# D * u added on GpSimd instead of by a transpose, and some loads asked for at other slots, in a Mamba layer with an FFN

## The chip, the cores and the metric

The kernel runs on one core of a Trainium2 chip. The metric is the device time of one execution in microseconds (us). TensorE is PE in the profile (PEld is its weight load), VectorE is DVE, ScalarE is ACT, GpSimd is POOL, and SyncE is SP, whose queue issues the DMAs.

## What is computed

Two sequences of 4096 tokens with 512 channels go through a Mamba layer and then an FFN with 4-bit weights, each with a layer norm before and after and a residual. The part that the change touches is the end of the Mamba layer:

```
h_in, gate = split(x_norm @ in_proj)                      # I = 1024 each
u   = silu(causal_conv(h_in) + conv_b)
ts, B, C = split(u @ x_proj, [128, 144])                  # N = 16 states
dt  = softplus(ts @ dt_proj + dt_b)
h_t = exp(dt * A) * h_(t-1) + dt * u * B                  # per channel and state
y   = sum over the 16 states of (h * C) + D * u
out = (y * silu(gate)) @ out_proj
```

All is float32 (matmuls in a mode in which two rounded halves of each operand are used, three products for one).

## The kernel before, in words

**Two stages.** The first stage, up to about 985 us, does the norm, in_proj, the convolution, x_proj and dt, group by group of 512 tokens (16 groups), and writes to device memory what the second needs: dt and D * u by channel (`dd_d`), dt * u with time on the partitions (`dT_d`), B, C, and silu(gate) (`g_d`; a part of the gates is left for the second stage, with inputs in `xg_d` and weights in `wg_d`).

**Slots.** The second stage is written as a list of slots. Time is cut into segments of 63 steps; a chunk is 4 segments, but the first chunk of each of the two sequences has one segment. A unit is one chunk for one block of 128 channels (8 blocks, `ib`). A unit has 2 slots for each segment, one for each half (`hf`) of the 16 states: 8 slots, or 2 in a one-segment chunk; 2080 slots in all. In a slot:

- TensorE makes the input of the scan two slots ahead, `make_b` (L938), two matmuls of the tile d (dt * u, from `dT_d`) with Bd, a diagonal matrix of B values that GpSimd makes (`make_bd`, L806). It goes into one of two PSUM tiles;
- ScalarE makes exp(dt * A) for the next unit (`make_exp`);
- VectorE runs the scan (L967), after a copy of the carried state (L966);
- after every second segment, GpSimd multiplies the states with C into `pr` (L979), 128 channels x 8 states x 126 steps, one product for each half of the states. h has two tiles, pr four;
- four slots later, `nsum` (L985) sums the states on TensorE: each of the 8 states of the half is transposed into the same PSUM tile yp and adds up there (L999), 16 transposes for both halves. A seventeenth (L1002) adds D * u, the tile du. VectorE multiplies with the gate (L1005), and the result goes to `y_d`.

**Beside the scans.** Matmul work runs between the slots: for each group of 512 tokens, out_proj of one group and the FFN of the one before (in the first two groups, the rest of the gates). `tail` yields it in small steps. A counter `pe` adds up an estimate of TensorE's time, and after each slot the loop takes steps until the counter has reached the slot's share of the group's `cost`; what is left at the end of the group is taken at once. An ordinary group has 128 slots:

```
cost += length * (2 * TB + (2 * NH + 1) * TT / NU)
...
while g >= 0 and pe[0] < cost * (slot + 1 - start[g]) / length and next(todo, 0) is None:
    pass
```

Here NH is 8, NU is 4, TB = 0.125, TT = 0.107, TM = 0.235 us. The group with the batch boundary in it has 144 slots.

**Order.** The order on PE, ACT, POOL and SP is that of the program; only VectorE's is chosen by the scheduler.

**Loads.** Functions handed to `at(slot, f)` run at that slot. `unit_steps` (L866) asks for dt and d of unit m at the slot in which unit m - 2 begins. In a one-segment chunk four units share a load; units 4 to 7 (`ib == NU`) of the second sequence's are asked for at the last unit of the chunk before, those of the very first chunk fall under the general rule. `load_gate` (L876) asks for du and the gate of unit k + 3 four slots after the last sum of unit k. `gates(hf, ...)` (L1025) asks for its 8 weight tiles of 256 KB at its start; `following` are the first loads of the next group's out_proj.

Of the kernel before, what the change touches and what calls it, by code (L numbers as in the profile page):

```python
# [25 lines left out]
def kernel(  # L26
# [7 lines left out]
    nc = tc.nc  # L34
# [7 lines left out]
    KH, KI, KF = H // P, I // P, HID // P  # L42
# [14 lines left out]
    NU = 4  # L57
# [648 lines left out]
    with ExitStack() as sb:  # L706
# [44 lines left out]
        NH = N // 2  # L751
# [14 lines left out]
        def first_of(c):  # L766
            nb, q, _ = chunks[c]
            return nb * T + V * q
# [97 lines left out]
        def unit_steps(m):  # L866

            b, n = (slots[m - 2], slots[m - 1] - slots[m - 2]) if m > 1 else (0, 0)
            c, ib = units[m]
            if chunks[c][2] == 1 and c and ib == NU:  # L870
                b, n = slots[c * KI - 1], NU * 2
            at(b, lambda: load_dt(m))
            for i in range(4):
                at(b + (1 + i if n > 2 else i // 2), lambda i=i: load_t4(m, i // 2, i % 2))
# [48 lines left out]
                nc.scalar.activation(dA[2 * (k % 2) + hf][:, :n_, m, 1:U], dtv, AF.Exp, scale=A[:, ib, n:n + 1])  # L923

        YA = 2
        prods, summed = {}, set()
        NE = 1
        hs = {}

# [22 lines left out]
        def scan(k, u, hf, slot):  # L952
            c, ib = units[k]
            q, n_ = chunks[c][1:]
            Cb = chunk[c][2]
            j, uu = divmod(u, 2)
            dAt = dA[2 * (k % 2) + hf]
            if hf == 0:
                hs["prev"] = last[ib] if u == 0 else hs["h"][:, :, 1 - uu, :, U - 1]
                if uu == 0:  # L960
                    hs["h"] = hp.tile([P, 2, 2, NH, U], F32, name=f"h{k}_{j}", tag="h")
            h = hs["h"][:, hf]
            b = bt.pop(slot)
            with tc.high_priority(offset=HP):
                if q + u:
                    nc.vector.tensor_copy(b[:, :, 0], hs["prev"][:, hf])  # L966
                scans.append(nc.vector.tensor_tensor_scan(  # L967
                    h[:, uu].rearrange("p n t -> p (n t)"),
                    dAt[:, u].rearrange("p n t -> p (n t)"),
                    b.rearrange("p n t -> p (n t)"),  # L970
                    0.0, ALU.mult, ALU.add,
                ))
            if u == n_ - 1 and hf == 1:
                nc.gpsimd.tensor_copy(last[ib], hs["h"][:, :, uu, :, U - 1])
            if uu == 1 or u == n_ - 1:
                pr = prp.tile([P, NH, 2 * V], F32, name=f"pr{k}_{j}_{hf}", tag="pr")
                f = 1 if q + u else 0
                to = pr[:, :, :(uu + 1) * (U - f)].rearrange("p n (u t) -> p u n t", t=U - f)
                nc.gpsimd.tensor_mul(to, h[:, :uu + 1, :, f:], Cb[j, hf][:, :uu + 1, :, f:])  # L979
                prods.setdefault(k, []).append(pr)  # L980
                sums.append((slot + NS, k, j, hf))

# [2 lines left out]
        def nsum(k, j, hf):  # L985

            c, ib = units[k]
            du, gt = glane[k]
            t, m = windows(c)[j]
            o_ = t - first_of(c)  # L990
            if hf == 0:
                i = nsums[0] % YA if now[0] < start[1] - 1 else None
                nsums[0] += 1
                yps[k, j] = (ps_w if i is None else ps_a).tile([P, P], F32, name=f"yp{c}_{ib}_{j}", tag="w" if i is None else f"a{i + 4 - YA}")
            yp = yps[k, j]
            pr = prods[k].pop(0)
            pe[0] += (NH + hf) * TT
            for n in range(NH):
                nc.tensor.matmul(yp[:m], pr[:, n, :m], ident, is_transpose=True, start=(hf == 0 and n == 0), stop=False)  # L999
            if hf == 0:  # L1000
                return
            nc.tensor.matmul(yp[:m], du[:, o_:o_ + m], ident, is_transpose=True, start=False, stop=True)  # L1002
            del yps[k, j]
            yt = sm.tile([P, P], F32, name=f"yt{c}_{ib}_{j}", tag="yt")
            nc.vector.tensor_mul(yt[:m], yp[:m], gt[:m, j])  # L1005

            def store():
                for g, o, at_, w in pieces(t, m):
                    nc.sync.dma_start(y_d[g][ib, o:o + w, :], yt[at_:at_ + w])
                    if o + w == G:  # L1010
                        summed.add((g, ib))

            at(now[0] + YD, store)
            if j == len(windows(c)) - 1:
                del lane[k], glane[k], prods[k]
                at(now[0] + 4, lambda: load_gate(k + 3))
# [5 lines left out]
        NS = 4  # L1022


        def gates(hf, following):  # L1025

            w = [c1.tile([P, KH, 512], FR, name=f"wg{hf}_{e}", tag="xh" if e == 0 else "xl") for e in range(2)]
            for kt in range(KH):
                for e in range(2):
                    nc.sync.dma_start(f32(w[e][:, kt]), wg_d[2 * hf + e][:, kt])  # L1030
            if hf:
                yield

            def x_in(g, j):
                t = wn_.tile([P, 2, KH, P], FR, name=f"xg{hf}_{g}_{j}", tag="wn")
                nc.sync.dma_start(f32(t), xg_d[g][j - JS])
                return t

            todo_ = [(g, j) for g in range(GS, NG - 1) for j in range(JS, J)]
            held = []  # L1040

            def let_go(f):

                while f in held:
                    held.pop(0)()

            if not hf:
                pe[0] += GD[0]
                yield
            raw, nxt = [], [x_in(*q) for q in todo_[:1 + hf]]  # L1050
            pe[0] += GD[1 + hf]
            yield
            for i, (g, j) in enumerate(todo_):
                t = nxt.pop(0)
                if i == 0 and not hf:
                    nxt.append(x_in(*todo_[1]))
                if i >= len(todo_) - 2:
                    following.send(None)
                if len(held) > 1:
                    let_go(held[0])  # L1060
                pm = (ps_a if hf else ps_w).tile([P, 512], F32, name=f"pz{hf}_{g}_{j}", tag=f"a{i % J}" if hf else "w")
                for kt in range(KH):
                    mm3b(pm, t[:, 0, kt], t[:, 1, kt], w[0][:, kt], w[1][:, kt], kt == 0, kt == KH - 1)
                    yield
                    if kt == 1 and i + 2 < len(todo_):
                        nxt.append(x_in(*todo_[i + 2]))
                z = row(f"z{hf}_{g}_{j}")
                held.append(lambda z=z, pm=pm: nc.scalar.copy(z, pm))
                at(now[0] + 2, lambda f=held[-1]: let_go(f))
                raw.append((g, j, z))  # L1070
                if len(raw) == GB or i == len(todo_) - 1:
                    def silu(raw=raw):
                        let_go(held[-1] if held else None)
                        for _, _, z in raw:
                            nc.scalar.activation(z, z, AF.Silu)

                    def store(raw=raw):
                        for g_, j_, z in raw:
                            nc.sync.dma_start(g_d[g_][4 * hf:4 * hf + 4, j_ * P:(j_ + 1) * P, :].rearrange("k p i -> p k i"), z.rearrange("p (k i) -> p k i", i=P))

                    at(now[0] + 3, silu)
                    at(now[0] + 5, store)
                    raw = []
            let_go(held[-1] if held else None)
            ahead[hf] = following.send(None)
            yield
# [7 lines left out]
        def row(nm):  # L1094
            return c2.tile([P, H], F32, name=nm, tag="xn", bufs=RB)
# [19 lines left out]
        def early(g):  # L1115

            ys = y_in(g, 0)
            w = w_in(g, 0)
            yield
            yn = y_in(g, 1)  # L1120
            wn = w_in(g, 1)
            yield
            tp = y_turn(g, 0, ys)
            yield split(c2, tp, [P, J, P], f"yy{g}_0", nc.scalar.copy, tag="h", bufs=HB), [w, wn], [yn]
# [260 lines left out]
        def tail(p):  # L1385

            if p == 0:
                yield from gates(0, early(0))
                return
            t, beside, late = turned.pop(p - 2, []), [], None  # L1390
            if p >= 2 and not t:
# [3 lines left out]
            ff = ffn(p - 2, t, early(p) if p < NG else None) if p >= 2 else iter(())  # L1395
            if p - 1 < NG:
                acc = new_acc(f"ca{p}")
                late = gates(1, early(1)) if p == 1 else None
                if late:
                    next(late)  # L1400
                yield from out_proj(p - 1, acc, ahead.pop(p - 1), beside, ff)
                assert not beside
                state[p - 1] = []
                norms(p - 1, acc, state[p - 1])
# [146 lines left out]
```

## Time and profile before

| | us |
|---|---|
| median of 3 runs (4635.6 to 4637.55) | 4637.4 |
| the profiled execution | 4638.11 |
| its span, first to last instruction | 4636.2 |
| first stage | about 985 |
| an ordinary group of 128 slots | 209.7 |
| TensorE busy in each 100 us from 1500 to 4400 | 97 to 99.6, but 89.8 from 2700 to 2800 |
| mean granted TensorE clock | 0.992 |

The whole page shows one busy figure for each engine over the span. A row of groups has the line, engine, operation, output and inputs with shapes, the count, then busy time and mean ns of one, then the idle time before it and what ended it. In a timeline, the first two figures are the start and the length in us, and a bracket gives idle time just before the row and who ended it. In a row of windows there are the stretch, its length, and for each engine the busy time with the number of instructions, then the granted clock, the DMA share and GB/s.

Other rows of use: `L1002 PE MATMUL yp<-ident,du` ran 528 times, its weight load 138 ns in the median; DVE's scan takes 1220 ns, its copy 166 ns.

### The profile page before, as it was taken

How to read it: one execution, taken by the hardware profiler on the slowest of the kernel's cores; microseconds unless marked ns; L12 is line 12 of the kernel's file. 1: busy time of each engine (PE TensorE's matmuls, PEld its weight loads, DVE VectorE, ACT ScalarE, POOL GpSimd, SP SyncE). 2: the span in 40 equal slices, each digit the busy share in tenths (PEclk: the TensorE clock that was granted, in tenths of full speed). 3: DMA queues.
4: the chain of work that ended last, by engine and by line, in shares of the span. 5: the costliest groups of instructions: out<-in, count | busy, mean ns of one | idle time of the engine just before them, and what ended most of it. 6: DMA issues, size and time to landing. Idle time of an engine off the chain costs nothing.

```text
span 4636.2 us, 84785 instructions
## 1 busy us (share of the span) xinstructions
PE 4479.6 (97%) x26613; PEld 3867.9 (83%) x26613; DVE 3843.9 (83%) x6273; ACT 3306.1 (71%) x7321; POOL 3275.0 (71%) x2360
## 2 busy tenths in 40 slices
PE   8999999979899999999999989999999999999999
PEld 6777777768788888888888878888888888888887
DVE  6677777759889999999989989899999999999931
ACT  5777777777688776867677667777686767767643
POOL 1333333349788888889888888888898989888820
PEclk9999999989999999999999999999999999999999
DMA  4888888778889787978888877879798978888765
GB/s 149 260 254 259 261 259 255 232 218 223 243 232 257 223 248 211 260 216 255 221 245 232 232 204 222 240 223 252 211 265 217 255 221 249 231 232 243 212 235 195
DMA packets 1137329, 1083.91 MB, mean 234 GB/s; under 512 B 140599, under 2 KB 910415, under 8 KB 1136888
## 3 DMA queue, kind: packets, MB, share of 16 engines
q1 hardware_dynamic: 1136888, 1078.49, 80.6%
q8 instruction: 220, 3.60, 0.3%
q14 instruction: 221, 1.81, 0.1%
HBM read 800.87 MB, written 277.29 MB: 233 GB/s over the span
## 4 chain that ended last, share of the span: by engine, by line
PE 75%; DVE 6%; DMA 6%; POOL 5%; ACT 4%; issue 3%; SPq 1%; DVEq 0%; POOLq 0%; ACTq 0%
PE yp L999 15%; PE b L949 8%; PE pu L99 5%; PE pu L100 5%; PE pu L101 5%; PE fa L99 5%; PE fa L100 5%; PE fa L101 4%; DVE h L967 3%; POOL pr L979 3%; PE pm L100 2%; PE pm L99 2%; PE pm L101 2%; POOL bd L809 2%; PE ca L99 1%
## 5 line engine op out<-in xcount | busy, mean ns | idle before, releaser
L979 POOL TENSOR_TENSOR pr<-h,cb 128x1008 f32<-128x1008 f32 (+1 forms) x1056 | 2454.0, 2336 | 469.9 <-DVE b L966 313.9
L967 DVE TENSOR_TENSOR_SCAN h<-dA,b 128x512 f32<-128x512 f32 x2080 | 2536.2, 1220 | 128.4 <-PE b L949 9.8
L923 ACT ACTIVATE dA<-dt,A 128x252 f32<-128x252 f32 x4096 | 1702.0, 496 | 163.6 <-DVE h L967 143.1
L999 PE MATMUL yp<-ident,pr 128*126 128x128 f32 (+1 forms) x8448 | 1104.9, 274 | 18.2 <-DVE xl L1265 6.8
L999 PEld LDWEIGHTS yp<-ident,pr 128*126 128x126 f32 (+1 forms) x8448 | 950.4, 140 | 28.5 <-issue 11.7
L949 PEld LDWEIGHTS b<-bd,d 128*128 128x128 f32 x4160 | 752.7, 190 | 209.2 <-issue 27.1
L949 PE MATMUL b<-bd,d 128*128 128x256 f32 x4160 | 875.4, 291 | 48.6 <-DVE h L967 15.7
L1312 ACT ACTIVATE pu<-pu,bu 128x512 f32<-128x512 f32 x256 | 168.8, 659 | 602.5 <-PE pu L101 602.5
L437 DVE SCALAR_TENSOR_TENSOR pm<-hin,cw,pm 128x512 f32<-128x512 f32 x384 | 288.4, 751 | 210.0 <-ACT pm L434 203.0
L99 PE MATMUL fa<-wn,hh 128*128 128x512 f32 x1024 | 421.1, 411 | 0.0
L99 PE MATMUL pu<-xh,wu 128*128 128x512 f32 x960 | 401.7, 418 | 5.0 <-DMA wu<-wu_d 4.8
L100 PE MATMUL fa<-wn,hh 128*128 128x512 f32 x1024 | 403.6, 394 | 0.0
L101 PE MATMUL fa<-wn,hl 128*128 128x512 f32 x1024 | 401.0, 392 | 0.0
L100 PE MATMUL pu<-xl,wu 128*128 128x512 f32 x960 | 378.3, 394 | 0.0
L101 PE MATMUL pu<-xh,wu 128*128 128x512 f32 x960 | 375.8, 392 | 0.0
L433 POOL COPY halo<-hin 128x3 f32<-128x3 f32 x128 | 28.1, 219 | 461.8 <-ACT hin L432 461.8
L966 DVE COPY b<-h 128x8 f32<-128x8 f32 x1536 | 254.7, 166 | 108.1 <-PE b L949 101.6
L1316 DVE TENSOR_TENSOR hl<-pu,hh 128x512 fp32r<-128x512 f32 x256 | 172.1, 672 | 152.5 <-ACT hh L1314 152.5
L809 POOL TENSOR_TENSOR bd<-dl,bp 128x512 fp32r<-128x512 f32 x260 | 273.1, 1060 | 1.1 <-DMA bp<-B_d 1.1
L101 PEld LDWEIGHTS fa<-wn,hl 128*128 128x128 f32 x1024 | 192.3, 188 | 44.8 <-DVE hl L1316 0.6
L101 PEld LDWEIGHTS pu<-xh,wu 128*128 128x128 f32 x960 | 180.4, 188 | 42.0
L100 PEld LDWEIGHTS fa<-wn,hh 128*128 128x128 f32 x1024 | 193.8, 189 | 20.3
(582 smaller groups left out, 7786.9 us busy)
## 6 DMA issues: line engine op xcount, KB each, us to landing
d<-dT_d SPq DMA_DIRECT2D x1040, 128.0 KB
wu<-wu_d SPq DMA_DIRECT2D x256, 512.0 KB
wn<-wn_d SPq DMA_DIRECT2D x256, 512.0 KB
cb<-C_d SPq DMA_DIRECT2D x128, 512.0 KB
wo<-wo_d SPq DMA_DIRECT2D x128, 512.0 KB
dd_d<-du SPq DMA_DIRECT2D x128, 256.0 KB
dd_d<-v SPq DMA_DIRECT2D x128, 256.0 KB
ys<-y_d SPq DMA_DIRECT2D x128, 256.0 KB
```

The costliest lines, as they stand in the source:

```text
L99: nc.tensor.matmul(ps, ah, bh, start=start, stop=False)
L100: nc.tensor.matmul(ps, ah, bl, start=False, stop=False)
L101: return nc.tensor.matmul(ps, al, bh, start=False, stop=stop)
L437: cv = nc.vector.scalar_tensor_tensor(pm, hin[:, k:k + G], cw[:, ib, k:k + 1], pm, ALU.mult, ALU.add)
L809: nc.gpsimd.tensor_mul(tb, dl.unsqueeze(1).to_broadcast([P, N, 32]), bp[:, w // 2, w % 2, :].unsqueeze(2).to_broadcast([P, N, 32]))
L923: nc.scalar.activation(dA[2 * (k % 2) + hf][:, :n_, m, 1:U], dtv, AF.Exp, scale=A[:, ib, n:n + 1])
L949: nc.tensor.matmul(b[:, :, v * 32:(v + 1) * 32], t4[:, u if l is None else l, v, :], Bd[2 * u + v][:, hf * NH:(hf + 1) * NH, :], start=Tru ...
L966: nc.vector.tensor_copy(b[:, :, 0], hs["prev"][:, hf])
L967: scans.append(nc.vector.tensor_tensor_scan(h[:, uu].rearrange("p n t -> p (n t)"), dAt[:, u].rearrange("p n t -> p (n t)"), b.rearrange(" ...
L979: nc.gpsimd.tensor_mul(to, h[:, :uu + 1, :, f:], Cb[j, hf][:, :uu + 1, :, f:])
L999: nc.tensor.matmul(yp[:m], pr[:, n, :m], ident, is_transpose=True, start=(hf == 0 and n == 0), stop=False)
L1316: nc.vector.tensor_sub(hl, pu, f32(hh))
```

## The change

The loads: dt and d of units 4 to 7 of the very first chunk are asked for at slots 0 and 1, and those of the first two units after a one-segment chunk at units 2 and 4 of the short chunk instead of units 6 and 7. The gate weights are now asked for through a list of four parts: all at once for the first half, and for the second half one part at a time, handed to out_proj as `beside`. The first loads of the next group are sent for in the middle of the last two gate blocks instead of at their start.

The sum: where du of the unit is already asked for when the second half's product is made, GpSimd adds du to state 0 of that product, in place, and the transpose of du is left out. The `cost` of the pacing is not edited.

```diff
             c, ib = units[m]
-            if chunks[c][2] == 1 and c and ib == NU:
-                b, n = slots[c * KI - 1], NU * 2
+            if chunks[c][2] == 1 and ib == NU:
+
+                b, n = (slots[c * KI - 1], NU * 2) if c else (0, 0)
+            elif c and chunks[c - 1][2] == 1 and ib < 2:
+                b = slots[m - 6 + ib]
             at(b, lambda: load_dt(m))
...
                 nc.gpsimd.tensor_mul(to, h[:, :uu + 1, :, f:], Cb[j, hf][:, :uu + 1, :, f:])
+                if hf and k in glane:
+                    added.add((k, j))
+                    t_, m_ = windows(c)[j]
+                    o_ = t_ - first_of(c)
+                    nc.gpsimd.tensor_add(pr[:, 0, :m_], pr[:, 0, :m_], glane[k][0][:, o_:o_ + m_])
...
-            pe[0] += (NH + hf) * TT
+            own = hf and (k, j) not in added
+            pe[0] += (NH + own) * TT
             for n in range(NH):
-                nc.tensor.matmul(yp[:m], pr[:, n, :m], ident, is_transpose=True, start=(hf == 0 and n == 0), stop=False)
+                nc.tensor.matmul(yp[:m], pr[:, n, :m], ident, is_transpose=True, start=(hf == 0 and n == 0), stop=(hf == 1 and not own and n == NH - 1))
             if hf == 0:
                 return
-            nc.tensor.matmul(yp[:m], du[:, o_:o_ + m], ident, is_transpose=True, start=False, stop=True)
+            if own:
+                nc.tensor.matmul(yp[:m], du[:, o_:o_ + m], ident, is_transpose=True, start=False, stop=True)
...
-        def gates(hf, following):
+        def gate_weights(hf):
             w = [c1.tile([P, KH, 512], FR, name=f"wg{hf}_{e}", tag="xh" if e == 0 else "xl") for e in range(2)]
-            for kt in range(KH):
+
+            def part(kt):
                 for e in range(2):
                     nc.sync.dma_start(f32(w[e][:, kt]), wg_d[2 * hf + e][:, kt])
-            if hf:
-                yield
+
+            return w, [lambda kt=kt: part(kt) for kt in range(KH)]
+
+        def gates(hf, w, following):
...
-                if i >= len(todo_) - 2:
-                    following.send(None)
...
                     if kt == 1 and i + 2 < len(todo_):
                         nxt.append(x_in(*todo_[i + 2]))
+                    elif kt == 1:
+                        following.send(None)
...
             if p == 0:
-                yield from gates(0, early(0))
+                w, loads = gate_weights(0)
+                for f in loads:
+                    f()
+                yield from gates(0, w, early(0))
...
-                late = gates(1, early(1)) if p == 1 else None
-                if late:
-                    next(late)
+                if p == 1:
+                    w, beside = gate_weights(1)
+                    late = gates(1, w, early(1))
                 yield from out_proj(p - 1, acc, ahead.pop(p - 1), beside, ff)
```

More of the change, by code (lines that the diff above doesn't have):

```diff
@@ L925 @@
         YA = 2
-        prods, summed = {}, set()
+        prods, summed, added = {}, set(), set()
         NE = 1
```

## Prediction

> **What bounds the kernel now.** I read the page's busy shares and chain first, then windows inside one period of the long stage, then the timeline of GpSimd and of TensorE in the fullest of them, then the rows by shape, and last the places where TensorE stands still at the start.
>
> ```profile
> PE 4479.6 (97%) x26613; PEld 3867.9 (83%) x26613; DVE 3843.9 (83%) x6273; ACT 3306.1 (71%) x7321; POOL 3275.0 (71%) x2360
> PE 75%; DVE 6%; DMA 6%; POOL 5%; ACT 4%; issue 3%; SPq 1%; DVEq 0%; POOLq 0%; ACTq 0%
> ```
>
> TensorE sets the end on average, and GpSimd looks a quarter free. But the average mixes stages. From 1420 to 4430 us the kernel repeats a group of 128 slots, 209.7 us each. Inside one group (2058 to 2268 us) the windows are:
>
> ```profile
> 2067.60:2089.50 21.90, 20.93 (x144) 18.70 (x143) 21.14 (x35) 20.54 (x48) 21.60 (x16) 1.00 0.89 258
> 2089.90:2151.20 61.30, 61.19 (x396) 54.65 (x395) 56.54 (x93) 46.05 (x110) 53.77 (x32) 1.00 0.95 271
> 2151.30:2203.90 52.60, 51.96 (x328) 46.23 (x327) 47.50 (x78) 39.37 (x94) 52.28 (x36) 1.00 0.84 238
> 2203.90:2268.10 64.20, 64.20 (x408) 57.40 (x407) 59.35 (x97) 40.72 (x95) 49.05 (x28) 1.00 0.68 190
> ```
>
> The columns are length, then busy time of PE, PEld, DVE, ACT, POOL. In the second and fourth window GpSimd has 8 and 15 us free. In the first and third it has 0.3 us free: next to the products with C it makes six and eight Bd tiles (L809) and the small steps and adds of the norms. I call these the two crowded stretches. TensorE still runs through them, because each product is ready some 4 us before its transposes. How far that reserve is eaten shows at the end of the second one:
>
> ```profile
> 2183.77 2.43 POOL L979 TENSOR_TENSOR pr<-h,cb 128x1008 f32<-128x1008 f32 x1
> 2186.11 1.10 POOL L809 TENSOR_TENSOR bd<-dl,bp 128x512 fp32r<-128x512 f32 x1
> ...
> 2188.81 1.04 POOL L809 TENSOR_TENSOR bd<-dl,bp 128x512 fp32r<-128x512 f32 x1
> 2189.82 7.00 POOL L979 TENSOR_TENSOR pr<-h,cb 128x1008 f32<-128x1008 f32 x3
> ...
> 2189.91 0.38 PE L949 MATMUL b<-bd,d 128*128 128x256 f32 x1 [0.64 <-POOL bd L809]
> ...
> 2195.10 0.90 PEld L999 LDWEIGHTS yp<-ident,pr 128*126 128x126 f32 x8
> ```
>
> The Bd tile that ends at 2189.85 is already late: TensorE waits 0.64 us for it. The product that ends at 2194.5 is the second of the run of three, and its transposes begin at 2195.10, 0.6 us later. In the first stretch the tightest product (2087.1 to 2089.5) leaves 0.9 us. Outside both stretches this reserve is 2.5 to 5.6 us.
>
> **The add on GpSimd.** 515 of the 528 sums get it; the first 13 keep their transpose, since the load of D * u is asked for after their product. It is 128x126 f32 (128x64 in one-segment chunks), two SBUF inputs. No such row exists; the neighbours are
>
> ```profile
> L979 POOL TENSOR_TENSOR pr<-h,cb 128x1008 f32<-128x1008 f32 x1024 | 2412.5, 2368 | 444.4 <-DVE b L966 313.9 <-PE b L949 106.4 <-DVE h L967 14.8
> L1218 POOL TENSOR_TENSOR xr<-xr,xi 128x512 f32<-128x512 f32 x64 | 82.8, 1294 | 10.9 <-DMA xi<-in_x 6.6 <-ACT xr L1197 4.4
> L1189 POOL TENSOR_TENSOR mnc<-mnc,rc 128x4 f32<-128x4 f32 x16 | 3.2, 202 | 1.3
> ```
>
> From 4 to 512 elements the slope is (1294-202)/508 = 2.15 ns, from 512 to 1008 it is (2368-1294)/496 = 2.17. So 126 elements take 202 + 122*2.15 = 464 ns. The add needs its own product finished, a wait on its own engine. L1189 waits in the same way for the row before it and shows 1.3 us idle over 16, 80 ns each. I take 0.55 us. Low end: 126/512 of the L1218 row, 0.32, with the wait 0.40. High end: the dearest tiny row, 128x1 at L1359, has a mean of 412 ns instead of 202, which gives 0.76.
>
> [...]
>
> Behind each add on GpSimd's queue stand the next product, the Bd tiles and the norm steps; TensorE waits for the first two. Outside the crowded stretches the add lies in free time, and its product still comes over 2 us early: nothing. In a crowded stretch every add moves all that follows.
> - First stretch: adds after the products of 2071, 2079 and 2087, 3*0.55 = 1.65, against 0.9 of reserve: 0.75 us stall.
> - Second stretch: adds after the products of 2149 (0.07 of it absorbed), 2155, 2162, 2170, 2176 and 2184 stand before the late Bd tile, which has no reserve: 0.48 + 5*0.55 = 3.2 us stall. The product of 2192 would need 3.8 - 0.6 = 3.2: the same stall, not a second one.
>
> Together 3.95 us a group (2.6 with an add of 0.40, 5.9 with 0.76). D * u must now be there before the add instead of before the last transpose, some 5 us sooner; TensorE waited for it once, 0.3 us, so it costs nothing; without that cover it would be a landing time of a few us.
>
> **The transpose taken away.** Eight weight loads of L999 take 0.90 us and start 0.109 us apart, so a group of 32 sums saves TensorE 32*0.109 = 3.5 us. Where does it appear? The pacing loop (L1490) hands out projection and FFN work until the counted cost reaches the slot's share of `cost`, and L1484 still counts 17 transposes. So each slot is filled up as before, 1.63 us, and the other work runs out early. By the code's own constants a group counted 209.08 before against a budget of 208.14, and counts 32*0.107 = 3.42 less now, 205.66: nothing is left for the last two slots. There TensorE needs only b products and transposes and runs ahead of VectorE, but just two PSUM tiles hold b. At the group's end the b of slot 648 was begun 1.41 us after the scan that freed its tile (2059.61); in the one-segment chunk, where TensorE does wait for scans, that distance is 0.12. So about 1.3 us can be run ahead; VectorE's scans there follow each other at 1.33 to 1.4 us and take in yy and xl rows of 0.6 to 0.67, so it can't follow much faster. I take 1.3 of the 3.5. Bounds: 0 (VectorE keeps the pace) and 3.5.
>
> Net per ordinary group: 3.95 - 1.3 = +2.65, in 13 groups +34. The group with the batch boundary hands out its rest in a flush, so it gains its 3.9 in full against 3.95: 0. In the first group (1041 to 1201) GpSimd is busy 145.6 of 160 us and gets 24 adds of 0.55, 13: full, I take +3 (0 to 8). In all +37.
>
> **The loads.**
>
> ```profile
> 1010.09 0.74 SPq L864 DMA_DIRECT2D d<-dT_d  x1
> 1015.51 0.56 PE L949 MATMUL b<-bd,d 128*128 128x256 f32 x1 [8.61 <-DMA d<-dT_d]
> 1211.78 3.67 SPq L1030 DMA_DIRECT2D wg<-wg_d  x8
> 1222.96 0.66 PE L1112 MATMUL ty<-ident,ys 128*128 128x128 f32 x4 [3.21 <-DMA ys<-y_d]
> 1253.72 0.66 PE L1112 MATMUL ty<-ident,ys 128*128 128x128 f32 x4 [3.39 <-DMA ys<-y_d]
> ```
>
> Units 4 to 7 of the first chunk get dt and d at slots 0 and 1, dt and half of d ahead of the eight gate-weight loads, instead of at slot 4 behind these and most stores of the last group: the 8.6 us wait and a 1.8 us one behind it go. All of them lie on the chain, since scans follow one another without slack from 1041 on. The granted clock was 0.56 from 989 to 1018 and 0.83 to 1041; less idling may give some of that back. I take -11 (0 to -18, the first idle to the restart at 1018). The gate weights of the second half (2 MB in one burst at 1211.8) are now spread over out_proj. Four waits of TensorE for ys behind that burst sum to 1.1 + 3.2 + 1.2 + 3.4 = 8.9 us; I take -7 (0 to -12). At the batch boundary TensorE's waits are for scans (9.0 us), none for dt or d: 0. Loads together -18.
>
> Sum, on the profiled execution of 4638.1 (span 4636.2, 1.9 around it; median of the runs 4637.4, so 0.7 above it): 4638 + 37 - 18 = **4657 us**.
>
> **Rivals.**
> - Balance: the two PSUM tiles don't hold TensorE back, so all 3.5 us appear, 13*(3.95 - 3.5) = +6, +3 in the first group, loads -20: 4627. For it: GpSimd's stalls come earlier and VectorE could use them to catch up. Against it: 2 slots are too short to use 3.5 us.
> - The other side, faster: GpSimd's queue has more room than its rows say (the page calls them rough), the add disappears in it and TensorE keeps its saving: 13*3.5 = 45, loads -20: 4573. It decides if an add costs less than about 0.2 us in the crowded stretches. Against it: the 0.64 us wait for Bd is there in each group already.
> - Worse: late products also hold h, which has two tiles, so scans wait too, or D * u lands late for the add: one more wait of 3 us a group, 4657 + 13*3 = 4696. Against it: only 2.5 us of waits of scans for products before.
>
> **How the numbers follow.** Forecast 0.60, balance 0.20, faster 0.10, worse 0.10. A measurement of this kernel tells 0.2%, 9 us, from no change. The forecast's own bounds are 4638 + 13*(2.6 - 1.3) + 3 - 30 = 4628 (add 0.40, both loads at their ends) to 4638 + 13*(5.9 - 1.3) + 3 - 12 = 4689 (add 0.76). Range 4624 to 4690: it takes in balance and leaves out the faster and the worse case. Slower: most of the forecast and all of the worse case, 0.64. Same: 0.16, from both middle cases. Faster: 0.20, half the balance and the faster case.
>
> **What would show it.** A row pr<-pr,du of about 465 ns; GpSimd over 95% in a group; TensorE waits of about 3 us for bd or pr once a group and under 1 us once more; a group of 211 to 213 us instead of 209.7; waits of b on scans in the last two slots; the 8.6 us wait gone. If groups shorten to 206, or adds take 0.3 us, I am wrong.

## The result and the profile after

The changed kernel takes 4688.3 us (median of 4 runs, 4683.6 to 4692.6) against 4637.5 for the kernel before on the same chip: ratio 1.0107 [1.0095, 1.0119], 51 us slower. The forecast was 4657, 20 slower. Sign and range held; 31 us are to be explained. The profiled execution of after took 4692.56 us, with a span of 4690.8.

The page of after, its busy line of TensorE and its chain:

```profile
PE 4462.0 (95%) x26098; PEld 3837.8 (82%) x26098; DVE 3835.0 (82%) x6273; ACT 3307.8 (71%) x7321; POOL 3497.5 (75%) x2875
...
PE 66%; POOL 9%; DMA 9%; DVE 6%; ACT 4%; issue 4%; SPq 2%; POOLq 0%; DVEq 0%; ACTq 0%
...
L987 POOL TENSOR_TENSOR pr<-pr,du 128x126 f32<-128x126 f32 (+1 forms) x515 | 224.7, 436 | 40.4
```

TensorE has 515 matmuls fewer and is busy for 18 us less, yet its share of the chain fell from 75% to 66%: GpSimd rose from 5 to 9%, DMA from 6 to 9%. The add costs what was forecast: 436 ns and 40.4/515 = 78 ns of idle before it, 0.515 us against 0.55.

Where the time went, by the starts of scans (one scan a slot; slot 0 is the first of the long stage), in the two profiled executions. "Ordinary" is the mean of the 13 groups of 128 slots:

| stretch | before us | after us | change | forecast |
|---|---|---|---|---|
| start to slot 0 | 989.0 | 995.2 | +6.2 | 0 |
| slots 0 to 134 | 215.8 | 216.9 | +1.1 | -8 |
| slots 134 to 262 | 221.3 | 212.8 | -8.5 | -7 |
| ordinary group, 13 of them | 210.8 | 215.3 | +4.5 each, +58 | +2.65 each, +34 |
| group with the batch boundary | 239.6 | 238.7 | -0.9 | 0 |
| from slot 2070 to the end | 229.6 | 228.2 | -1.4 | 0 |

The rows add up to +54.6, the difference of the two profiled spans; the medians differ by 51. The stage before slot 0 isn't touched by the change; over the 14 kernels profiled here slot 0 came between 985.9 and 996.7. So the ordinary groups hold the loss. The 209.7 us ahead of the prediction was one such group; the mean of the 13 was 210.8. In the waits of TensorE from 1500 to 4400 us (who waits for whom: us in all, times, longest) the kernel before has

```profile
PE b L949 <- DVE h L967: 10.2, 11, 2.9
PE b L949 <- POOL bd L809: 8.8, 14, 0.8
...
PE pu L99 <- DMA wu<-wu_d: 4.0, 3, 1.8
...
PE yp L999 <- POOL pr L979: 0.3, 1, 0.3
```

and the kernel after

```profile
PE yp L1008 <- POOL pr L987: 29.1, 29, 1.5
PE pu L99 <- DMA wu<-wu_d: 20.6, 10, 3.8
PE b L952 <- POOL bd L809: 19.7, 26, 1.8
PE b L952 <- DVE h L970: 15.1, 21, 1.2
PE b L952 <- PE b L952: 9.0, 9, 1.0
```

Waits for the add (L987) and for late Bd tiles were forecast. The second row was not: TensorE waits for the FFN weights `wu`, which the change doesn't touch. And these waits don't add up to the loss by themselves. The windows of one ordinary group of after (length, busy time of PE, PEld, DVE, ACT, POOL, then granted clock, DMA share, GB/s) show what else there is:

```profile
2066.10:2282.00 215.90, 207.18 (x1300) 183.93 (x1300) 192.34 (x317) 152.96 (x364) 196.07 (x146) 0.99 0.79 230
2074.10:2097.10 23.00, 22.34 (x153) 20.01 (x151) 21.58 (x37) 19.07 (x43) 22.51 (x18) 1.00 1.09 287
...
2120.80:2123.80 3.00, 0.27 (x2) 0.00 (x0) 1.07 (x1) 3.00 (x11) 3.00 (x3) 1.00 1.04 294
2123.80:2127.20 3.40, 3.32 (x12) 3.06 (x13) 1.13 (x2) 2.01 (x6) 3.32 (x4) 0.50 1.06 336
...
2158.00:2211.00 53.00, 50.07 (x312) 44.00 (x311) 45.34 (x74) 38.04 (x91) 52.20 (x40) 1.00 0.85 245
2211.00:2280.80 69.80, 69.80 (x440) 62.28 (x439) 64.06 (x107) 42.38 (x98) 59.99 (x42) 1.00 0.65 194
2280.80:2284.20 3.40, 1.62 (x13) 1.27 (x12) 3.33 (x6) 3.40 (x11) 2.61 (x4) 1.00 0.09 22
2284.20:2287.60 3.40, 3.40 (x16) 3.11 (x14) 1.86 (x3) 2.92 (x9) 3.40 (x3) 0.50 0.72 203
```

The two crowded stretches (second and fifth row) lose 0.7 and 2.9 us, and GpSimd is at 98% in both, as forecast (over the whole group at 91%, where over 95% was forecast). The third row is the wait for `wu`, the seventh the end of the group. After each of these the granted clock is 0.50 for 3.4 us: TensorE is "busy" all the time there, at half speed. I call such a stretch a spell. In a mean clock of 0.987 against 0.992 this hides; between 1500 and 4400 us there is one spell before (6.8 us, at the batch boundary) and 14 after (47.8 us). Each 3.4 us at half speed is counted here as 1.7 us lost; the experiments below bear that out.

The timeline of GpSimd and TensorE of after in the second crowded stretch (start, length, engine, row, in brackets the idle time before it):

```profile
2197.06 2.37 POOL L982 TENSOR_TENSOR pr<-h,cb 128x1008 f32<-128x1008 f32 x1
...
2199.51 0.46 POOL L987 TENSOR_TENSOR pr<-pr,du 128x126 f32<-128x126 f32 x1
...
2200.02 1.09 PE L1008 MATMUL yp<-ident,pr 128*126 128x128 f32 x8 [1.46 <-POOL pr L987]
...
2201.58 2.05 POOL L809 TENSOR_TENSOR bd<-dl,bp 128x512 fp32r<-128x512 f32 x2
...
2202.68 0.38 PE L952 MATMUL b<-bd,d 128*128 128x256 f32 x1 [0.85 <-POOL bd L809]
...
2203.68 0.39 PE L952 MATMUL b<-bd,d 128*128 128x256 f32 x1 [0.62 <-POOL bd L809]
```

This is the forecast stall: the add ends at 2199.97, its transposes start 0.05 us later, and the two Bd tiles behind the norm steps come late too. Together 2.93 us, where the kernel before had 0.64: +2.3, against a forecast of 3.2. In the first crowded stretch TensorE had two short waits before, 0.41 and 0.56 us, both for VectorE. After, it has one of 0.55 for VectorE and one of 0.62 for the add: +0.2 against 0.75.

The timeline of TensorE in after around the wait for `wu`:

```profile
2120.68 0.39 PE L101 MATMUL ca<-wo,yy_7l 128*128 128x512 f32 x1
2123.88 0.76 PE L99 MATMUL pu<-xh,wu 128*128 128x512 f32 x1 [2.81 <-DMA wu<-wu_d]
2124.45 0.63 PE L100 MATMUL pu<-xl,wu 128*128 128x512 f32 x1
2124.87 0.63 PE L101 MATMUL pu<-xh,wu 128*128 128x512 f32 x1
...
2127.56 0.40 PE L100 MATMUL pu<-xl,wu 128*128 128x512 f32 x1
```

The same 128x512 matmul has a span of 0.63 us in the spell and 0.40 after it; starts are 0.43 us apart instead of 0.23. The wait itself comes from TensorE being early. Where it waited for the second `wu` tile of an ordinary group, the tile came 5.3 to 6.2 us after it was asked for in before and 4.4 to 6.8 us in after, so the load isn't clearly slower. But TensorE was ready for it 5.9 us after the asking in before (mean of the 13 groups) and 4.2 us in after. With the pacing told of 16 transposes (below) it is 6.1 again.

The end of the group in after, where the work handed out has run dry:

```profile
2279.78 0.40 PE L952 MATMUL b<-bd,d 128*128 128x256 f32 x2
2280.02 1.04 PE L1008 MATMUL yp<-ident,pr 128*126 128x128 f32 x8
2280.81 0.48 PE L952 MATMUL b<-bd,d 128*128 128x256 f32 x2
2282.07 0.47 PE L952 MATMUL b<-bd,d 128*128 128x256 f32 x2 [0.78 <-DVE h L970]
2283.55 0.48 PE L952 MATMUL b<-bd,d 128*128 128x256 f32 x2 [1.00 <-DVE b L969]
2283.87 1.57 PE L1008 MATMUL yp<-ident,pr 128*126 128x128 f32 x8
```

TensorE has nothing but b products and transposes, and waits 0.78 and 1.00 us for one of the two b tiles, here put down to VectorE's scan and copy. In most other groups the profile puts the second wait down to TensorE's own b row (9.0 us in the waits above). That was forecast as a lost saving; that a spell of half clock follows (the last row, 1.57 us instead of 1.04) was not.

### The profile page after: what moved, and what is told of

Same layout as the page of the kernel before. It is cut to its first block, busy times and chain, and to the rows that moved or that the text cites. A ratio compares the mean times of both kernels' runs of the same rounds, so it can differ in the third digit from the quotient of the medians.

```text
span 4690.8 us, 84330 instructions
## 1 busy us (share of the span) xinstructions
PE 4462.0 (95%) x26098; PEld 3837.8 (82%) x26098; DVE 3835.0 (82%) x6273; ACT 3307.8 (71%) x7321; POOL 3497.5 (75%) x2875
## 3 DMA queue, kind: packets, MB, share of 16 engines
q14 instruction: 227, 1.86, 0.1%
## 4 chain that ended last, share of the span: by engine, by line
PE 66%; POOL 9%; DMA 9%; DVE 6%; ACT 4%; issue 4%; SPq 2%; POOLq 0%; DVEq 0%; ACTq 0%
PE yp L1008 13%; PE b L952 7%; POOL pr L982 5%; PE pu L99 4%; PE fa L99 4%; PE fa L100 4%; PE fa L101 4%; PE pu L100 4%; PE pu L101 4%; DVE h L970 3%; POOL bd L809 2%; PE pm L100 2%; PE pm L99 2%; PE pm L101 2%; DMA wu<-wu_d 1%
## 5 line engine op out<-in xcount | busy, mean ns | idle before, releaser
L437 DVE SCALAR_TENSOR_TENSOR pm<-hin,cw,pm 128x512 f32<-128x512 f32 x384 | 288.0, 750 | 212.8 <-ACT pm L434 205.8
L987 POOL TENSOR_TENSOR pr<-pr,du 128x126 f32<-128x126 f32 (+1 forms) x515 | 224.7, 436 | 40.4
```

The source lines that it names most:

```text
L437: cv = nc.vector.scalar_tensor_tensor(pm, hin[:, k:k + G], cw[:, ib, k:k + 1], pm, ALU.mult, ALU.add)
L987: nc.gpsimd.tensor_add(pr[:, 0, :m_], pr[:, 0, :m_], glane[k][0][:, o_:o_ + m_])
```

## The experiments

All ratios are against the kernel before on the same chip (4635.7 to 4639.6 us in the four sets of runs, so a difference in us between rows of two sets is good to some 4 us). "Group" is the mean ordinary group. TensorE's idle time and the loss to half clock (half of each spell's length) are per group, spells are those from 1500 to 4400 us. The kernel before has 210.8 us, 2.2 idle, no loss. Groups, idle and spells are read from one profiled execution of each kernel.

| kernel | us | ratio | group | idle | half clock | spells |
|---|---|---|---|---|---|---|
| after | 4688.3 | 1.0107 [1.0095, 1.0119] | 215.3 | 7.4 | 1.83 | 14 |
| loads only | 4628.8 | 0.9987 [0.9978, 0.9995] | 210.6 | 2.0 | 0 | 1 |
| sum only, old loads | 4680.1 | 1.0098 [1.0079, 1.0117] | 214.5 | 7.0 | 1.44 | 10 |
| after, pacing told of 16 | 4669.0 | 1.0071 [1.0057, 1.0085] | 213.4 | 5.2 | 1.96 | 12 |
| 16 transposes, no add | 4647.1 | 1.0024 [1.0014, 1.0035] | 212.5 | 5.1 | 1.70 | 13 |
| the same, pacing told | 4608.1 | 0.9932 [0.9917, 0.9946] | 209.2 | 3.6 | 0.13 | 2 |
| add and 17 transposes | 4696.4 | 1.0121 [1.0104, 1.0137] | 215.5 | 4.8 | 1.70 | 12 |
| add of 16 columns | 4665.1 | 1.0052 [1.0037, 1.0067] | 213.5 | 5.9 | 1.57 | 12 |
| add in units 1 to 5 | 4656.0 | 1.0036 [1.0024, 1.0048] | 212.8 | 4.5 | 1.57 | 11 |
| short stall | 4644.4 | 1.0007 [0.9998, 1.0017] | 211.5 | 2.9 | 0 | 1 |
| long stall | 4680.1 | 1.0085 [1.0072, 1.0099] | 214.5 | 4.6 | 1.57 | 11 |
| loads and early du | 4633.3 | 0.9989 [0.9980, 0.9999] | 210.9 | 2.2 | 0.13 | 2 |
| add in units 1 to 4 | 4647.3 | 1.0018 [1.0009, 1.0028] | 211.8 | 3.5 | 1.44 | 14 |

Take idle and half clock off the group, and what is left hardly depends on the spells: 208.3 to 209.0 us in the six kernels with 17 transposes, before among them, and 205.5 to 206.2 in the six with 16. So half a spell's length is a fair price for it, and the transposes taken away are worth some 2.5 to 3 us a group, not the 3.5 of the forecast.

**The two halves of the change apart.** Loads only, from after:

```diff
                 nc.gpsimd.tensor_mul(to, h[:, :uu + 1, :, f:], Cb[j, hf][:, :uu + 1, :, f:])
-                if hf and k in glane:
-                    added.add((k, j))
...
-                    nc.gpsimd.tensor_add(pr[:, 0, :m_], pr[:, 0, :m_], glane[k][0][:, o_:o_ + m_])
```

> The changed kernel with the loads at their new slots, but with the seventeenth transpose and without the add. Theory (the sum makes the loss, the loads gain): the profile after shows the group that had the burst of gate weights 8.5 us shorter and nothing gained in the first one, since a wait of 8.3 us for du took the place of the one for d, so 4637 - 8 = about 4629 us, ordinary groups back at 209 to 211 us with no half-clock spell in them. Rival (the loads at their new slots disturb the whole run, the add costs little): 4660 or more, groups of 213 us and more, waits for wu in each.

Measured 4628.8, 6.9 us below the kernel before in the same set. The other half alone, the sum with the old loads, is the same block and the `own` lines put into the kernel before.

> The kernel before with the add on GpSimd and 16 transposes, loads as before. Theory: ordinary groups as in the changed kernel, 214 to 215 us, so 4637 + 13*4.5 = 4696 us, some 8 more than the changed kernel. Rival (loads make the loss): below 4650 us.

Measured 4680.1, well above the rival's 4650 but 16 below the 4696 expected, which had the old loads cost 8 us on top of after. The loss is all in the sum. The loads gain 7 us with the old sum. With the new one no gain shows: after is 8 us above the sum alone, and the ratios of the two, 1.0107 and 1.0098, overlap in their intervals.

**The pacing.** After, with the cost of a group counted by 16 transposes:

```diff
-                    cost += length * (2 * TB + (2 * NH + 1) * TT / NU)
+                    cost += length * (2 * TB + 2 * NH * TT / NU)
```

> The changed kernel with the pacing told of 16 transposes instead of 17, so that the other matmul work is spread evenly to the end of the group. Theory: the two waits of b for scans at the group's end (1.7 us) go, and with them the half-clock spell (1.8 us a group) that follows them, and the run-ahead that made TensorE arrive early at its second wu tile; the stalls on GpSimd grow by the same 1 to 2 us, because each slot is shorter: 4665 to 4690 us, fewer than 8 half-clock spells after 1500 us instead of 16. Rival (GpSimd alone decides): the stalls take up all of it, 4685 to 4695 us, with as many spells.

4669.0: the time lies where it was expected, 19 us below after, and the waits at the end of the group are gone, as is the wait for `wu` (0.1 us a group instead of 1.6). But 12 spells stay, not under 8: with the work spread evenly TensorE meets the late Bd tile with 2.3 us in one piece, and the half clock follows that. TensorE's waits from 1500 to 4400 us:

```profile
PE b L952 <- POOL bd L809: 30.8, 15, 2.3
...
PE pu L99 <- DMA wu<-wu_d: 1.3, 2, 1.0
```

**The shorter sum without the add.** This kernel leaves D * u out of 515 of the 528 sums, so that what is timed is 16 transposes and no work on GpSimd in their place:

```diff
                 if hf and k in glane:
                     added.add((k, j))
-                    t_, m_ = windows(c)[j]
-                    o_ = t_ - first_of(c)
-                    nc.gpsimd.tensor_add(pr[:, 0, :m_], pr[:, 0, :m_], glane[k][0][:, o_:o_ + m_])
```

> The changed kernel without the add and without the seventeenth transpose, so D * u is left out of 515 of the 528 sums: what the shorter sum is worth when GpSimd does nothing for it. Theory: no more stalls on products or Bd than before; the saving of 3.5 us a group is realised by half (1.7 us of waits for scans in the last two slots), less what half-clock spells after these waits take: 4629 - 13*1.7 = about 4607 us, up to 4625 with a spell in each group. Rival (the add is free and the empty last slots make the loss): no faster than the changed kernel, 4680 us or more.

4647.1, neither the 4607 to 4625 of the theory nor the rival's 4680, and this miss is the finding of the study. Taking 515 transposes away, with nothing put in their place, makes the kernel 18 us slower than loads only. The waits of TensorE from 1500 to 4400 us in loads only, and then in this kernel:

```profile
PE b L952 <- DVE h L970: 10.2, 11, 2.9
PE b L952 <- POOL bd L809: 9.0, 14, 0.9
...
PE pu L99 <- DMA wu<-wu_d: 1.9, 2, 1.0
```

```profile
PE pu L99 <- DMA wu<-wu_d: 27.2, 11, 3.8
PE b L952 <- DVE h L970: 16.7, 23, 1.7
PE b L952 <- POOL bd L809: 8.9, 14, 1.5
PE b L952 <- PE b L952: 7.0, 7, 1.0
```

GpSimd's waits stay as they were (8.9 us for Bd, 9.0 in loads only), while those for `wu` and for the b tiles appear. Each group does 2.9 us less work, idles 3.1 more and loses 1.7 to half clock. VectorE's order, which the scheduler chooses, differs as well: from that of loads only at 1665 of 6273 places here, at 67 in the next kernel. How much of the loss comes with that order and how much with TensorE's early running was not separated.

**The same with the pacing told.** As above and the cost line of the pacing experiment; D * u is left out of the same sums. This was to tell whether the pacing is what turns the saving into a loss.

> As the one without add and without the seventeenth transpose (D * u left out of 515 of 528 sums), but with the pacing told of 16 transposes. Theory: it is the uneven pacing, with its waits for scans in the last two slots, its early need of the second wu tile and the half-clock spells behind both, that ate the saving; paced evenly no wait reaches 1.5 us, at most 3 spells after 1500 us, ordinary groups of 207 us, 4629 - 14*3.5 = about 4580 us. Rival (VectorE or the loads set the pace as soon as TensorE has less to do): no faster than 4625 us, groups of 210 us and more with waits of b for scans all over.

4608.1, 39 us faster than the one above by one line that does no arithmetic on the chip, and 21 faster than loads only; two spells are left, and the wait for `wu` is 8.6 us in place of 27.2. In kind it is what was expected, in size less: I had hoped for 4580. The saving had is about 1.4 us a group (210.6 to 209.2), not 3.5; the best groups take 207.0.

**The add without the shorter sum.** Here du is added on GpSimd and its transpose is kept as well, so D * u is counted twice in 515 sums:

```diff
                 if hf and k in glane:
-                    added.add((k, j))
```

> The changed kernel with the add on GpSimd and the seventeenth transpose as well, so D * u is added twice in 515 sums: GpSimd's part alone, on the pacing of before. Theory: the add stalls TensorE in the crowded stretches by some 3 us a group, and a spell at half clock adds up to 1.7: 4629 + 14*3 = 4671 up to 4695 us, no wait for scans at the group's end, none for the second wu tile. Rival (the add is hidden, the pacing makes the whole loss): under 4645 us.

4696.4, 67.6 above loads only: the add by itself costs a group 4.9 us, 2.8 as waits and 1.7 as half clock, with the pacing even. In one group the waits of the second stretch are 0.80 us for the add and 2.27 for the Bd tile, 3.07 in place of 0.94 in loads only.

**A shorter add.** Only 16 of up to 126 columns are added, so most of D * u is left out of those sums. One theory had the loss grow in proportion to the add's length (4671), one had a reserve that swallows a short one (4660), and one had only the wait between the two GpSimd instructions count, not the length (4680 or more).

```diff
-                    nc.gpsimd.tensor_add(pr[:, 0, :m_], pr[:, 0, :m_], glane[k][0][:, o_:o_ + m_])
+                    nc.gpsimd.tensor_add(pr[:, 0, :16], pr[:, 0, :16], glane[k][0][:, o_:o_ + 16])
```

> The changed kernel with an add of 16 columns instead of 126, so D * u is left out for most steps: the dose. The add should take about 0.24 us instead of 0.44, with its wait 0.31 instead of 0.52. Theory with a reserve: first stretch 3*0.31 = 0.9 just fits, second 0.24 + 5*0.31 = 1.8 against 3.0, so 1.9 us a group less than in the changed kernel: 4660 us. Rival without a reserve (each add counts in proportion): 4647 + 0.6*40 = 4671 us. Rival (not the length but the wait between the two GpSimd instructions counts): 4680 us or more.

The row of the add in this kernel:

```profile
L987 POOL TENSOR_TENSOR pr<-pr,du 128x16 f32<-128x16 f32 x515 | 114.1, 222 | 40.4
```

An eighth of the elements still costs 222 + 78 = 0.30 us against 0.515. The time, 4665.1, speaks against the third and lies between the other two, so between these it decides nothing: 41.3 us lie between no add and the whole add, and 0.30/0.515 of that would be 24, where 18 were measured.

**Half clock by itself.** If the spells and not only the waits cost, a wait that makes no spell must cost its length and one that does must cost more. Two kernels from loads only repeat Bd products once a group in front of the last Bd tile of the second stretch; nothing but delay is put in. The short one repeats a quarter of one, the long one two whole ones:

```diff
         def make_bd(c, w):
...
+            if w == 7 and c > 4 and c % 2 == int(c > 17):
+                for _ in range(2):
+                    nc.gpsimd.tensor_mul(tb[:, :16], dl.unsqueeze(1).to_broadcast([P, 16, 32]), bp[:, w // 2, w % 2, :16].unsqueeze(2).to_broadcast([P, 16, 32]))
```

> The kernel with the new loads alone, in which the last Bd tile before the late one in the second crowded stretch is preceded, once a group, by one more product of a quarter of its size (128x128, some 0.4 us) that it overwrites: a pure delay on GpSimd. [...] Rival (any wait costs a spell, or a spell has another cause): spells in most groups, 4655 us, or none and no change.

> As the short delay, but with two more products of full size (2.2 us with their waits). Theory: TensorE waits some 2.9 us for Bd, 2.3 more than before, and a spell at half clock follows in nearly each ordinary group, 1.7 us more: 4.0 a group, 4629 + 14*4 = 4685 us, 11 to 14 spells after 1500 us. Rival (the spells cost nothing of their own, or come from something else than waiting): 14*2.3 = 32, so 4661 us, or no more than 3 spells.

The wait for Bd from 1500 to 4400 us in the short and in the long one:

```profile
PE b L955 <- POOL bd L812: 15.8, 15, 1.2
```

```profile
PE b L955 <- POOL bd L812: 41.1, 15, 3.2
```

The short one has waits of 1.2 us and one spell, the one at the batch boundary: a group costs 0.9 us more and idles 0.9 more, where I had expected 0.5 and no spell, and the time of 4644.4 lies between the 4636 of that (4629 + 14*0.5) and the rival's 4655. What separates them is the absence of spells in the ordinary groups. The long one has waits of 2.9 us, 11 spells, and a group costs 3.9 more while it idles 2.6 more; the rest is the half clock's 1.57. The time of 4680.1 is nearer the 4685 of the theory than the 4661 that the waits' length alone gives. From the short to the long one, both of one set, it is 35.7 us, and the idle time of 13 groups grows by 22. What follows the wait, in the timeline of the long one:

```profile
2405.84 0.36 PE L955 MATMUL b<-bd,d 128*128 128x256 f32 x1
2409.13 0.58 PE L955 MATMUL b<-bd,d 128*128 128x256 f32 x1 [2.92 <-POOL bd L812]
2409.51 0.63 PE L99 MATMUL pu<-xh,wu 128*128 128x512 f32 x1
...
2412.47 0.40 PE L99 MATMUL pu<-xh,wu 128*128 128x512 f32 x1
```

**Can the add be kept where GpSimd has room?** Units are numbered 0 to 7 in a chunk; the crowded stretches lie at the ends of chunks. The add is made in units 1 to 5 only, then in 1 to 4 only, with the counted cost to match (16.375 and 16.5 transposes). The edit of the second:

```diff
-                if hf and k in glane:
+                if hf and k in glane and 1 <= ib <= 4:
...
-                    cost += length * (2 * TB + (2 * NH + 1) * TT / NU)
+                    cost += length * (2 * TB + (2 * NH + 0.5) * TT / NU)
```

> The add only in units 1 to 5 of each chunk, away from the crowded stretches around a chunk's start; units 0, 6 and 7 keep the seventeenth transpose; the pacing counts 16.375. 20 of 32 sums in a group have the add. Theory: no stall on GpSimd beyond those of before, 20*0.109 = 2.2 us a group saved and all of it realised: 4629 - 14*2.2 = about 4598 us, faster than both kernels. Rival (adds ahead of a stretch eat the reserve too): 4625 us or more, waits for bd of over 1 us in each group.

> The add only in units 1 to 4 of each chunk, pacing of 16.5 transposes. Theory: the unit-5 adds stood just ahead of the second stretch and made the Bd wait 1.65 us; without them it is at most 1.0. The other wait of 2.5 us (a PSUM tile that VectorE frees late, by its own order) stays or goes with VectorE's order, which can't be told beforehand: 4615 us if it goes, 4650 if it stays. Rival (the adds of units 1 to 4 stall by themselves): waits of transposes for pr of over 1 us in each group.

4656.0 and 4647.3, neither below the kernel before; the first was expected at 4598. With units 1 to 5 the wait for the Bd tile stays (21.3 us from 1500 to 4400 us, up to 1.7 at once), as its rival had it. With units 1 to 4 the stall of the second stretch is gone (0.75 us a group for b, as in loads only). But some 18 us into each group TensorE now waits for VectorE:

```profile
PE yp L1008 <- DVE xl L1278: 31.0, 13, 2.5
```

The row xl frees a PSUM tile that the transposes need, and in the order that the kernel's scheduler chose for these two kernels VectorE does the first xl of a group one scan later than in loads only. So once a group 2.5 us of idle, and a spell of half clock after it. The second kernel was made to see whether this wait goes with the sixth unit; it doesn't. Whether the idea is worth something with VectorE's order held is open; it wasn't tried.

**The wait for du at the front.** In after the 8.6 us wait for d is gone, but another took its place: one of the 13 transposes of du that are kept (L1012) waits for its load. TensorE's waits from 985 to 1190 us, in before and then in after:

```profile
PE b L949 <- DMA d<-dT_d: 12.1, 4, 8.6
```

```profile
PE yp L1012 <- DMA du<-dd_d: 8.3, 1, 8.3
```

In loads only it is 6.4 us, and the profile names the gate's load, which is asked for together with du. Loads only, with du and the gates of units 4 to 7 of the first chunk asked for early as well:

```diff
-        for m in range(3):
+        for m in range(5):
             at(m, lambda m=m: load_gate(m))
...
-                at(now[0] + 4, lambda: load_gate(k + 3))
+                at(now[0] + 4, lambda: load_gate(k + 3) if k > 1 else None)
```

> The new loads alone, and du and the gate of units 4 to 7 of the first chunk asked for at slot 4 too. Theory: the wait of 6.4 us for du in the first group, which took the place of the wait for d, goes, and with the idle time some of the half-clock time around it: 4629 - 5 = about 4624 us, faster than both kernels. Rival (the first group is bound by what comes later): 4629 us, unchanged.

The wait for du is gone, but the time is 4633.3 where 4624 was expected, and its ratio of 0.9989 is that of loads only. The slots 0 to 134 take 210.4 us (loads only 209.7): two waits for d of 2.4 and 1.3 us and one of 2.6 for a copy of VectorE come instead.

## Why the prediction was right in sign and short by 31 us

- **The range** held by luck: its upper end of 4690 stood for an add of 0.76 us, and the add took 0.515.
- **The add's price** was right: 0.515 us against 0.55.
- **The stalls** were in the right places and too large when read as waits: per group +2.3 us in the second crowded stretch and +0.2 in the first, against 3.2 and 0.75. Priced alone, by add and 17 transposes against loads only, the add costs 4.9 us, 2.8 of it as waits and 1.7 as half clock, for which the forecast had nothing.
- **"I take 1.3 of the 3.5"** is the step that failed. Reasoning and place were right (the pacing counts 17, the work runs out, two PSUM tiles hold TensorE), but the step let the worst case be a saving of nothing. Against loads only, the shorter sum cost 18 us (4647.1 to 4628.8) where 13 * 1.3 = 17 were to be gained. Two things were left out. TensorE, being early all through the group, also meets the `wu` load before it lands (1.3 us a group more in after). And every wait was priced at its own length, while the waits that the step allows bring the half clock.
- **The half clock** is what separates the sums. Idle time grew by 5.2 us a group and the work shrank by 2.5, which gives +2.7, close to the forecast's +2.65. That is partly luck: waits for GpSimd grew by some 3 where 3.95 were forecast, and the other waits ate nearly all of the 2.5 saved where 1.3 were to be left. The half clock comes on top with 1.83, and 13 * 1.83 = 24 us. By the stretches of the table the forecast misses 35.5 of the 54.6 us: 24 in the ordinary groups, 9 in slots 0 to 134, 6 ahead of slot 0, where the change has no part; the other rows give 4 back.
- **How the parts share the loss** depends on the order in which they are put in, since they trigger the same spells. From loads only (4628.8): first the sum +18, then the add +41; or first the add +68, then the sum -8. With the pacing told, the sum gains 21 without the add and 27 with it. So the edit missing from the change, the cost line, is worth 19 us in after, and even then the add loses (4669.0).
- **The loads** gave -7, not -18. At the front -11 was forecast; slots 0 to 134 take 209.7 us in loads only, a gain of 6. The rest went to the wait for du, since I had not followed the loads past the wait for d; and with that wait gone too (early du, 210.4) the next waits set the same end. In after they take 216.9. The adds don't explain that by themselves, since with add and 17 transposes it is 212.7; the cause is open. For the burst of gate weights -7 was forecast, and the group of slots 134 to 262 did get 8.5 shorter in after. Whether that is the loads' is open: loads only takes 221.2 there, as before, but the two stall kernels, whose added delays start later, take 216.2 and 214.5, and the sum with the old loads 212.3. One profile of each can't tell a gain of 7 from this scatter. And of the four waits behind the burst that were put down to ys, the profile names one (1.1 us) as issue.
- **The batch boundary group** changed by -0.9, forecast 0; its parts were not taken apart.
- **The rivals:** balance needed all of the saving to appear; the experiments without the add exclude it as long as the pacing counts 17. The add did not disappear. The worse case (4696) is nearer in time than the forecast, by 8 us to 31, and a part of it came: scans now wait for products, in VectorE's waits from 1500 to 4400 us of before and then of after:

```profile
DVE h L967 <- POOL pr L979: 1.0, 2, 0.6
```

```profile
DVE h L970 <- POOL pr L982: 30.2, 49, 1.4
```

That is 2.2 us a group, where one more wait of 3 was forecast. But these waits hardly reach TensorE: its own waits for scans grow from 10.2 to 15.1 us over the same time, and the one of 0.69 us at 2199 lies beside TensorE's own 1.46 for the add. Nor are they all the add's: without an add (16 transposes) they are 14.1 us. What they add to the time by themselves was not tried. The add never waited for D * u: none of the 515 had more than 0.15 us of idle time before it.

Of the kernels that compute all of it, only loads only (0.9987 of before) and the same with early du (0.9989) are below before, and these two can't be told apart.

## What to carry to other kernels

Where the clock drops after waits, as TensorE's did here (a granted clock of 0.50 for 3.4 us after a wait of 2.81), a wait has a second price, so ask not only how long TensorE will idle but how much of the idle falls together: in the two stall kernels 1.2 us at once brought no spell in an ordinary group, and 2.9 us one in 10 of 13. Work taken from a paced engine is not a saving until the pacing knows of it: change the cost that the pacing counts in the same edit, and look for loads that were just in time. And an add on an engine that is 71% busy is dear if the stretch in which it stands is at 99%: here it cost 4.9 us a group.

## What the runs showed of the hardware

**Half clock after waits.** Between 1500 and 4400 us each of the 14 spells of after lasted 3.4 us, and the one of before 6.8, with a wait of 2.94 us for a scan. Around slot 0, where TensorE was busy for 13.2 of 29 us in before and the granted clock over these was 0.56, one lasted 20.5. Of the 14 of after, 7 follow the two waits at the group's end (0.77 and 1.00 us, to 0.01), 5 a wait for `wu` (1.86 to 3.79 us) and 2 the waits for the add and the late Bd tiles (1.45, 0.86 and 0.62 us, to 0.01). But the same two waits at the group's end brought none at 1851 and 2066 us, nor did the 1.46, 0.85 and 0.62 us of the second crowded stretch at 2200. The waits of 1.2 us in the short stall brought none in an ordinary group, those of 2.9 us in the long one brought one in 10 of 13. What tells a wait with a spell from the same wait without one was not shown.

**The add's price on GpSimd.** 16 columns took 222 ns and 126 took 436 (a mean with some of 64 columns), about 2 ns for each further one, so by an estimate from these two rows nearly 0.2 us of each add didn't depend on its size, nor did the 78 ns before it (40.4 us over 515 in both).
